# An LSTM with a residual on one core: moving the first groups of products between the plain products, and building the input-weight sums from one another

## The chip, the cores and the metric

The kernel runs on one core of one Trainium2 chip. The metric is the device time of one execution in microseconds (us); the figure for a kernel is the median of its timed runs. Names of the engines: TensorE is PE in the profile, VectorE is DVE, ScalarE is ACT, GpSimd is POOL, SyncE is SP.

## What is computed

The reference is an LSTM over 512 time steps for a batch of 32, with 512 inputs and 512 hidden units, and a residual sum:

```python
def lstm_forward(x, h0, Wx, Wh, b):          # x (32, 512, 512), Wx and Wh (512, 2048)
    xW = jnp.einsum('ntd,dg->ntg', x, Wx) + b
    def step(carry, xw_t):
        prev_h, prev_c = carry
        a = xw_t + prev_h @ Wh
        i, f, o = sigmoid(a[:, :H]), sigmoid(a[:, H:2*H]), sigmoid(a[:, 2*H:3*H])
        g = jnp.tanh(a[:, 3*H:])
        next_c = f * prev_c + i * g
        next_h = o * jnp.tanh(next_c)
        return (next_h, next_c), next_h
    ...
return x + hs
```

All numbers are float32.

## The kernel before

There are two kinds of matmul work. The recurrence, `h_part(k)` (L624), multiplies the state by Wh once per time step and adds into one of two PSUM banks, `gates[0]` and `gates[1]`, which alternate by step. ACT seeds those banks with the input part of the step (`seed_first`, `seed_last`, L611 and L615). `cell(k)` (L637) then makes the new state: sigmoids and tanh on ACT, products on DVE, a transpose of the state on DVE (L659) for which the next recurrence waits.

The input part, x times Wx, is made ahead of time in three ways:

- **Plain products**, `direct(t, bank)` (L557): one time step at full cost, into a whole PSUM bank; `keep_direct` (L573) has DVE add the bias and move the result to SBUF. Steps 0 to 7 and the last 16 steps are made so.
- **Units**, in the head (steps 8 to 39): a unit is eight time steps of one column block of Wx. It is done with seven block products in place of eight (a Strassen-Winograd scheme), each over two halves k. It needs sums of the x blocks (`inner_sums`, L236 to L239, by `prepare`) and sums of four columns of a Wx block (`t_sums`, L160 to L162).
- **Jobs of superblocks**, from step 40 on: 24 steps in a block, 20 jobs each. These use a second, outer scheme that multiplies sums of x blocks by sums of Wx blocks. The Wx sums are constant, so they are made once: `make_factors(n)` (L201 for the additions of blocks, L210 to L213 for the four inner differences), and then stored to DRAM by SP (L207) and fetched again when a job needs them. Fourteen of the twenty are sums of two or more blocks.

The products of units and jobs are spread over **windows**. A unit or job that begins in window w has its products in windows w to w + 4; `products(v)` (L369) issues all products of window v, and `evacuate(v)` moves finished parts out of PSUM: ACT copies (L397, L401, L408, L409, L432) and DVE additions (L404, L410) that read and rewrite the same banks. The 16 units start at windows 0, 1, 2, 3, 4, 5, 6, 8, 9, 11, 12, 14, 15, 17, 18 and 20. Which windows belong to step k is written out by hand:

```python
def windows_of(k):
    if k < 0:
        return [0]
    return [2 * k + 1, 2 * k + 2] if k < 3 else [k + 4]
```

so steps 0, 1 and 2 have two windows each, one behind the other, and every later step has one. In a step, the order of issue is `h_part`, then for each window `evacuate`, `run_due`, `products`, `fetch`, and the cell behind the first window.

DVE's deferrable work (the Wx sums, and in the steady part the x sums) lies in a list sorted by the window in which it is due. `run_due(v, room)` issues what is due, and then what fits into a room given in columns (5000 in the head, an operation costs its columns plus 160). The tiles of Wx sums in the making rotate through a ring of three (`wa`) and a ring of four (`wb`); a tile's buffer is free again when its store has been done.

The order at the start, before step 0: six warm-up matmuls (L745) on zeros, plain products of steps 0 to 3 interleaved over the four quarters of the inputs, the `t_sums` of all eight Wx blocks, the x sums for window 0 (`prepare(0)`), the bias additions of steps 0 to 3, plain products of steps 4 to 7 into four free banks with `run_due(0, 2800)` behind each, the seeds, `products(0)`.

At the end, in the window `FIRST_TAIL - 5`, SP asks for two Wx blocks (0 and 5) again, because their room had been used for other things, and for the last two rows of x (L732 and L119), in one burst.

The whole order is fixed by the program: no scheduler moves an instruction on its engine.

Of the kernel before, what the change touches and what calls it, by code (L numbers as in the profile page):

```python
# [9 lines left out]
F32 = mybir.dt.float32  # L10
# [4 lines left out]
P = 128  # L15
B = 32
T = 512
NJ = 4
G = 4
IFG = 3 * P  # L20
ROW = 8
NROWS = T // ROW
C = 256
# [11 lines left out]
R = len(A_OF)  # L35
# [15 lines left out]
UNITS = [(i, j) for i in range(1, HEAD // ROW) for j in range(NJ)]  # L51


def windows_of(k):

    if k < 0:
        return [0]
    return [2 * k + 1, 2 * k + 2] if k < 3 else [k + 4]


START = windows_of(HEAD - LEAD)[0]
# [14 lines left out]
def kernel(  # L76
# [39 lines left out]
    def load_row(i, a=0, b=ROW):  # L116
        if i not in rows:
            rows[i] = xpool.tile([P, ROW, NJ, B], F32, name=f"row_{i}", tag="row")
        nc.sync.dma_start(  # L119
            out=rows[i][:, a:b].rearrange("p t q b -> p (t q b)"),  # L120
            in_=x[i][:, a * P : b * P],
        )
# [55 lines left out]
    def ring(n, name):  # L178
        return (
            rpool.tile([P, 3, C], F32, name=f"wa_{name}", tag="wa", bufs=3),  # L180
            rpool.tile([P, 4, C], F32, name=f"wb_{name}", tag="wb", bufs=4),
        )

    def make_factors(n):
        tiles = []
        (first, s0), *rest = B_OF[n]
        assert s0 > 0
        v = nc.vector

        def dst(part):  # L190
            if not tiles:
                tiles.extend(ring(n, f"make_{n}"))
            return tiles[1][:, 0:3] if part.start else tiles[0][:, 0:1]

        ops = []
        for part in (slice(0, 1), slice(1, 4)):
            for m, (b, sign) in enumerate(rest):

                def add(part=part, m=m, b=b, fn=v.tensor_add if sign > 0 else v.tensor_sub):
                    to = dst(part)  # L200
                    fn(to, to if m else raw[first][:, part], raw[b][:, part])  # L201

                ops.append(((part.stop - part.start) * C, add))

        def keep():
            for to, part in zip(kept[n], tiles):
                nc.sync.dma_start(out=to, in_=part.rearrange("p n c -> p (n c)"))  # L207

        ops += [
            (C, lambda: v.tensor_sub(tiles[0][:, 1], tiles[1][:, 0], tiles[0][:, 0])),  # L210
            (C, lambda: v.tensor_sub(tiles[1][:, 3], tiles[1][:, 2], tiles[1][:, 0])),
            (C, lambda: v.tensor_sub(tiles[0][:, 2], tiles[1][:, 2], tiles[0][:, 1])),
            (C, lambda: v.tensor_sub(tiles[1][:, 0], tiles[1][:, 1], tiles[0][:, 2])),  # L213
            (0, keep),
        ]
        return ops

    def push_factors():
        done = []
        ops = [op for n in range(R) if len(B_OF[n]) > 1 for op in make_factors(n)]  # L220
# [35 lines left out]
    def run_due(v, room):  # L256

        i = 0
        while i < len(due):
            window, _, columns, fn, ready = due[i]  # L260
            if window > v and (columns + FIXED > room or not ready(v)):
                i += 1
                continue
            assert ready(window)
            due.pop(i)
            fn()
            room -= columns + FIXED
            i = 0
# [283 lines left out]
    def direct(t, bank, qs=range(4)):  # L552
        i, a = divmod(t, ROW)
        for q in qs:
            k, e = divmod(q, 2)
            for j in range(NJ):
                nc.tensor.matmul(  # L557
                    flat(bank)[j * B : (j + 1) * B],
                    rows[i][:, a, q],
                    raw[NJ * k + j][:, 2 * e : 2 * e + 2].rearrange("p n c -> p (n c)"),  # L560
                    start=q == 0,
                    stop=True,
                    skip_group_check=True,
                )

    def keep_direct(t, bank, room=None):
        if room is not None:
            xw[t] = room
        elif t < 4:
            xw[t] = upool.tile([P, G * P], F32, name=f"xw_{t}", tag="xw", bufs=4)  # L570
        else:
            xw[t] = node_free[t - 4].rearrange("p t e b -> p (t e b)")
        nc.vector.tensor_add(xw[t], flat(bank), bias_sb)  # L573
# [144 lines left out]
    def fetch(v):  # L718

        job = jobs.get(v + 2)  # L720
        if job and job.w >= START and len(B_OF[job.kind[1]]) > 1:
            job.ring = [rpool.tile([P, 3, C], F32, name=f"wa_{job.w}", tag="wa", bufs=3), None]
            nc.sync.dma_start(out=job.ring[0].rearrange("p n c -> p (n c)"), in_=kept[job.kind[1]][0])
        job = jobs.get(v)
        if job and job.w >= START and len(B_OF[job.kind[1]]) > 1:
            job.ring[1] = rpool.tile([P, 4, C], F32, name=f"wb_{job.w}", tag="wb", bufs=4)
            nc.sync.dma_start(out=job.ring[1].rearrange("p n c -> p (n c)"), in_=kept[job.kind[1]][1])
        if v == FIRST_TAIL - 5:
            for i in range(8):
                if i not in single:  # L730
                    raw[i] = rpool.tile([P, 4, C], F32, name=f"raw_again_{i}", tag="wb", bufs=4)
                    nc.sync.dma_start(out=raw[i].rearrange("p n c -> p (n c)"), in_=wx[i])  # L732
            for i in range(END // ROW, T // ROW):
                load_row(i)
        sb, rest = divmod(v + 6 - START, PER)
        if v + 6 in UNIT_AT[2 * NJ :: NJ]:
            load_row(3 + UNIT_AT[2 * NJ :: NJ].index(v + 6))
        if rest < MO and 0 <= sb < NSB:
            load_row(HEAD // ROW + MO * sb + (0, 2, 1)[rest])

    with tc.manual_schedule():
        warm = work.tile([P, G, P], F32, name="warm", tag="s")
        nc.scalar.activation(warm[:, 0], c_init, AF.Sigmoid)
        for m in range(6):
            nc.tensor.matmul(  # L745
                pps[0][0:B].rearrange("p n c -> p (n c)"),
                c_init[:, 0:B],
                c_init.unsqueeze(1).to_broadcast([P, 4, P]),
                start=True,
                stop=True,  # L750
            )
# [105 lines left out]
```

## Time and profile before

| | |
|---|---|
| median of 3 runs | 3162.43 us (3160.52 to 3162.44) |
| the profiled execution's own time | 3159.27 us |
| its span, first to last instruction | 3157.5 us |
| mean granted TensorE clock | 0.998 |
| busy: PE, DVE, ACT, POOL | 99%, 70%, 51%, 29% |

The profile is of one execution. Busy shares are of the span. In a timeline row stand the start, the length, engine, line, operation, output and input tiles, shape, the count of instructions merged into the row and, in brackets, the idle time before it and what ended that. A float32 matmul shows as two records.

### The profile page before, as it was taken

The numbers are of one execution on the slowest core, as the hardware profiler recorded it, in microseconds if no ns is written. First come the engines' busy times: TensorE is split into PE (matmuls) and PEld (weight loads), VectorE is DVE, ScalarE is ACT, GpSimd is POOL, SyncE is SP. The second block draws the span as 40 slices with busy tenths as digits, with TensorE's granted clock in tenths as the row PEclk, the third lists the DMA queues.
The fourth block names the chain that finished last, engine by engine and source line by source line (L and its number), as shares of the span: only waits on it lengthen the run. The fifth ranks groups of instructions, "written<-read, shape, count | busy, mean of one in ns | idle before, by whom it ended". The sixth has DMA issues, their size and how long they took to land.

```text
span 3157.5 us, 133431 instructions
## 1 busy us (share of the span) xinstructions
PE 3125.9 (99%) x56620; PEld 2002.8 (63%) x56620; DVE 2198.7 (70%) x6139; ACT 1605.6 (51%) x4842; POOL 915.9 (29%) x1001
## 2 busy tenths in 40 slices
PE   9999999999999999999999999999999999999999
PEld 3666666666666666666666666666666666666544
DVE  7736777777676777777776777776777767677433
ACT  2445555555555555555555555555555555555333
POOL 0122333233233323232332323232333323232320
PEclk9999999999999999999999999999999999999999
DMA  6555666666665756767676757667576667576410
GB/s 237 180 169 187 227 209 207 219 193 227 210 225 186 244 188 216 225 189 227 193 225 207 229 184 240 193 216 226 185 231 199 224 207 236 175 233 195 153 62 25
DMA packets 316085, 631.64 MB, mean 200 GB/s; under 512 B 41952, under 2 KB 107744, under 8 KB 314976
## 3 DMA queue, kind: packets, MB, share of 16 engines
q1 hardware_dynamic: 315344, 623.09, 61.4%
q8 instruction: 446, 7.31, 1.0%
q14 instruction: 151, 1.24, 0.1%
q10 hardware_dynamic: 144, 0.01, 0.0%
HBM read 448.60 MB, written 174.33 MB: 197 GB/s over the span
## 4 chain that ended last, share of the span: by engine, by line
PE 85%; DVE 8%; ACT 3%; DMA 2%; issue 1%; SPq 1%; DVEq 0%; POOL 0%; ACTq 0%; POOLq 0%
PE gates L624 50%; PE pp L369 15%; PE acc L369 14%; PE p L369 5%; DMA xw<-raw_sb 1%; PE pp L557 1%; DMA xw<-slot 1%; DVE node L304 1%; ACT pp L408 1%; SPq L426 1%; DVE wb_make L201 1%; PE acc L557 1%; DVE c L652 1%; ACT ig L653 1%; DVE fc L654 0%
## 5 line engine op out<-in xcount | busy, mean ns | idle before, releaser
L624 PE MATMUL gates<-wh_sb,ht 128*32 128x384 f32 x32704 | 1873.2, 380 | 20.0 <-DVE ht L659 19.3
L624 PEld LDWEIGHTS gates<-wh_sb,ht 128*32 128x32 f32 x32704 | 1120.8, 110 | 804.6 <-issue 672.6
L663 POOL TENSOR_TENSOR oc<-xr,ht 128x128 f32<-128x128 f32 x509 | 299.5, 588 | 2146.6 <-DVE ht L659 2132.5
L605 POOL TENSOR_TENSOR xw<-xw,bias_sb 128x512 f32<-128x512 f32 x488 | 634.1, 1299 | 76.9 <-DMA xw<-xw 36.2
L647 ACT ACTIVATE s<-gates 128x256 f32<-128x256 f32 x512 | 197.7, 386 | 799.2 <-PE gates L624 793.1
L410 DVE TENSOR_TENSOR pp<-acc,p 128x256 f32<-128x256 f32 x396 | 171.0, 432 | 251.4 <-ACT pp L409 237.7
L650 DVE TENSOR_TENSOR fc<-s,c 128x128 f32<-128x128 f32 x511 | 149.9, 293 | 238.7 <-ACT s L647 234.6
L654 DVE TENSOR_TENSOR fc<-s,ig 128x128 f32<-128x128 f32 x512 | 149.5, 292 | 192.7 <-ACT ig L653 192.7
L408 ACT COPY pp<-pu 128x512 f32<-128x512 f32 x396 | 237.1, 599 | 47.8 <-DVE slot L516 18.5
L611 ACT COPY gates<-xw 128x384 f32<-128x384 f32 x492 | 232.7, 473 | 23.0 <-DVE xw L573 21.4
L369 PE MATMUL pp<-wb,node 128*32 128x256 f32 x3040 | 243.6, 379 | 0.0
L649 ACT ACTIVATE s<-gates 128x128 f32<-128x128 f32 x512 | 142.3, 278 | 189.2 <-PE gates L624 189.2
L653 ACT ACTIVATE ig<-c 128x128 f32<-128x128 f32 x512 | 158.6, 310 | 140.8 <-DVE c L652 114.2
L409 ACT COPY pp<-acc 128x256 f32<-128x256 f32 x396 | 142.2, 359 | 142.8 <-DVE slot L516 69.1
L659 DVE STREAM_TRANSPOSE ht<-fc 128x128 f32<-128x128 f32 x511 | 159.1, 311 | 53.8 <-DVE fc L654 0.5
L404 DVE TENSOR_TENSOR pu<-acc,p 128x256 f32<-128x256 f32 x396 | 162.4, 410 | 27.7 <-ACT p L401 27.7
L397 ACT COPY pu<-acc 128x256 f32<-128x256 f32 x396 | 147.3, 372 | 47.3 <-PE acc L369 45.0
L369 PE MATMUL acc<-wa,s 128*32 128x256 f32 x2128 | 170.6, 379 | 0.0
L369 PE MATMUL acc<-wb,s 128*32 128x256 f32 x2128 | 170.5, 379 | 0.0
L369 PE MATMUL pp<-wb,s 128*32 128x256 f32 x2128 | 170.5, 379 | 0.0
L369 PE MATMUL p<-wa,s 128*32 128x256 f32 x2128 | 170.5, 379 | 0.0
L401 ACT COPY p<-p 128x256 f32<-128x256 f32 x396 | 149.6, 378 | 26.7 <-PE p L369 20.5
(144 smaller groups left out, 4072.5 us busy)
## 6 DMA issues: line engine op xcount, KB each, us to landing
wb<-keep_b SPq DMA_DIRECT2D x266, 512.0 KB, 5.4
xw<-xw SPq DMA_DIRECT2D x488, 256.0 KB, 4.0
wa<-keep_a SPq DMA_DIRECT2D x266, 384.0 KB, 4.8
xw<-slot SPq DMA_DIRECT2D x624, 128.0 KB, 3.2
xr<-in_x_dram SPq DMA_DIRECT2D x256, 128.0 KB, 3.1
out_dram<-oc SPq DMA_DIRECT2D x255, 128.0 KB, 2.1
row<-in_x_dram SPq DMA_DIRECT2D x63, 512.0 KB, 6.8
xw<-raw_sb SPq DMA_DIRECT2D x252, 128.0 KB, 3.4
```

What stands on the lines that cost most here:

```text
L369: nc.tensor.matmul(dst[t * B : (t + 1) * B], a[:, t], w, start=s in (1, 5) and m == 0, stop=True, skip_group_check=True,)
L404: nc.vector.tensor_add(job.pu[:, 1], job.acc, job.p5)
L408: nc.scalar.copy(job.pp[0], job.pu)
L410: nc.vector.tensor_add(job.pp[1][:, 1], job.acc, job.p5)
L605: nc.gpsimd.tensor_add(xw[t], xw[t], bias_sb)
L611: nc.scalar.copy(gates[t % 2][:, 0:IFG], xw[t][:, 0:IFG])
L624: nc.tensor.matmul(g[j * B : (j + 1) * B, cols], state["ht"][:, k, :], wh_sb[:, k, j, cols], start=False, stop=True, skip_group_check=True,)
L647: nc.scalar.activation(s[:, 0:2], g[:, 0:2], AF.Sigmoid)
L650: nc.vector.tensor_mul(fc, s[:, 1], state["c"])
L653: nc.scalar.activation(tc_t, c, AF.Tanh)
L659: nc.vector.transpose(ht.rearrange("p q b -> p (q b)"), h)
L663: (nc.gpsimd if t < T - 3 else nc.vector).tensor_add(state["oc"][:, tt % 2], xr[t][:, tt % 2], ht)
```

## The change

- `windows_of(k)` is `[k + 4]` for every step. Windows 0 to 3 are issued ahead of step 0: `products(0)` behind the plain products of step 3, and windows 1, 2 and 3 behind the plain products of steps 4, 5 and 6 (each with its `evacuate`, `run_due` and `fetch`).
- The plain products of steps 4 to 7 go into `gates[0]` and `gates[1]` in turn, not into four other banks. `run_due` there has a room of 2400.
- The x sums of window 0 come after the `t_sums` of five Wx blocks; the other three follow.
- The warm-up has 24 matmuls over four column strips of `pps[2]`, not 6 in one strip of `pps[0]`.
- The Wx sums are built from one another, as a list `B_OPS` written by hand has it: 15 additions of blocks, not 31. A number -1 - n in the list stands for the four inner differences of sum n and its store. The order in which the sums are made and stored changes with it.
- At the end, the two rows of x are asked for in windows `FIRST_TAIL - 10` and `- 8`, the two Wx blocks in `FIRST_TAIL - 5` and `- 3`.

From step 12 or so on up to the reloads the order of the instructions on each engine is the same as before.

```diff
+B_OPS = [
+    (0, "add", 0, 4),
+    (3, "add", 8, 3),
+    (11, "sub", 2, 8),
+    -1,
+    (1, "add", 8 + 3, 7),
+    -1 - 3,
+    (12, "add", 8 + 11, 6),
...
+]
 def windows_of(k):
-    if k < 0:
-        return [0]
-    return [2 * k + 1, 2 * k + 2] if k < 3 else [k + 4]
+    return [k + 4]
...
-    def make_factors(n):
-        tiles = []
-        (first, s0), *rest = B_OF[n]
...
+    def push_factors():
+        v = nc.vector
+        made, ops, done = {}, [], []
+        def outer(n, how, a, b, part):
+            if n not in made:
+                made[n] = ring(n, f"make_{n}")
+            def source(u):
+                if u < 8:
+                    return raw[u][:, part]
+                return made[u - 8][1][:, 0:3] if part.start else made[u - 8][0][:, 0:1]
+            (v.tensor_add if how == "add" else v.tensor_sub)(source(8 + n), source(a), source(b))
...
+        for op in B_OPS:
+            if isinstance(op, int):
+                for z in ((1, 4, 0), (7, 6, 4), (2, 6, 1), (4, 5, 2)):
+                    ops.append((C, lambda n=-1 - op, z=z: inner(n, *z)))
+                ops.append((0, lambda n=-1 - op: keep(n)))
+            else:
+                for part in (slice(0, 1), slice(1, 4)):
+                    ops.append(((part.stop - part.start) * C, lambda op=op, part=part: outer(*op, part)))
...
-        if v == FIRST_TAIL - 5:
-            for i in range(8):
-                if i not in single:
-                    raw[i] = rpool.tile([P, 4, C], F32, name=f"raw_again_{i}", tag="wb", bufs=4)
-                    nc.sync.dma_start(out=raw[i].rearrange("p n c -> p (n c)"), in_=wx[i])
-            for i in range(END // ROW, T // ROW):
-                load_row(i)
+        if v in (FIRST_TAIL - 10, FIRST_TAIL - 8):
+            load_row(END // ROW + (v - FIRST_TAIL + 10) // 2)
+        if v in (FIRST_TAIL - 5, FIRST_TAIL - 3):
+            i = [i for i in range(8) if i not in single][(v - FIRST_TAIL + 5) // 2]
+            raw[i] = rpool.tile([P, 4, C], F32, name=f"raw_again_{i}", tag="wb", bufs=4)
+            nc.sync.dma_start(out=raw[i].rearrange("p n c -> p (n c)"), in_=wx[i])
...
-        for m in range(6):
+        for m in range(6 * NJ):
             nc.tensor.matmul(
-                pps[0][0:B].rearrange("p n c -> p (n c)"),
+                pps[2][m % NJ * B : (m % NJ + 1) * B].rearrange("p n c -> p (n c)"),
...
-        for i in range(8):
+        for i in range(5):
             for op in t_sums(i):
                 op()
         for op in prepare(0):
             op()
+        products(0)
+        for i in range(5, 8):
+            for op in t_sums(i):
+                op()
         push_factors()
         for t in range(4):
             keep_direct(t, firsts[t])
-        for t, bank in zip(range(4, ROW), (pps[2], accs[0], accs[1], p5)):
-            direct(t, bank)
-            run_due(0, 2800)
-            keep_direct(t, bank)
+        for v, t in enumerate(range(4, ROW), 1):
+            direct(t, gates[t % 2])
+            for op in prepare(v):
+                op()
+            if v < 4:
+                evacuate(v)
+            run_due(0, 2400)
+            keep_direct(t, gates[t % 2])
+            if v < 4:
+                products(v)
+                fetch(v)
         seed_first(0)
         seed_last(0)
         seed_first(1)
-        products(0)
-        for op in prepare(1):
-            op()
```

More of the change, by code (lines that the diff above doesn't have):

```diff
@@ L51, with check_sums @@
 UNITS = [(i, j) for i in range(1, HEAD // ROW) for j in range(NJ)]
+B_OPS = [
[6 more added lines that the diff above has]
+    (12, "add", 8 + 11, 6),
+    -1 - 11,
+    -1 - 1,
+    -1 - 12,
+    (4, "add", 1, 5),
+    (10, "add", 8 + 4, 6),
+    -1 - 4,
+    (8, "add", 8 + 10, 2),
+    -1 - 10,
+    (15, "add", 8 + 8, 3),
+    -1 - 8,
+    (17, "add", 8 + 15, 7),
+    -1 - 15,
+    -1 - 17,
+    (5, "add", 0, 3),
+    -1 - 5,
+    (13, "sub", 2, 0),
+    -1 - 13,
+    (19, "add", 5, 6),
+    -1 - 19,
+    (16, "add", 1, 2),
+    (16, "add", 8 + 16, 3),
+    -1 - 16,
+]
+def check_sums():
+    value = {b: {b: 1} for b in range(8)}
+    for op in B_OPS:
+        if isinstance(op, int):
+            continue
+        n, how, a, b = op
+        total = dict(value[a])
+        for block, sign in value[b].items():
+            total[block] = total.get(block, 0) + (sign if how == "add" else -sign)
+        value[8 + n] = {block: sign for block, sign in total.items() if sign}
+    for n, terms in enumerate(B_OF):
+        assert len(terms) == 1 or value[8 + n] == dict(terms)
+check_sums()
 def windows_of(k):
-    if k < 0:
-        return [0]
-    return [2 * k + 1, 2 * k + 2] if k < 3 else [k + 4]
+    return [k + 4]
 START = windows_of(HEAD - LEAD)[0]
@@ L182, in ring @@
         )
-    def make_factors(n):
-        tiles = []
-        (first, s0), *rest = B_OF[n]
-        assert s0 > 0
+    def push_factors():
         v = nc.vector
[L190 to L206, printed above, removed]
-                nc.sync.dma_start(out=to, in_=part.rearrange("p n c -> p (n c)"))
[L209 to L216, printed above, removed]
@@ new lines, in inner, with keep @@
+        def inner(n, to, a, b):
+            to, a, b = (made[n][z // 4][:, z % 4] for z in (to, a, b))
+            v.tensor_sub(to, a, b)
+        def keep(n):
+            for to, part in zip(kept[n], made[n]):
+                nc.sync.dma_start(out=to, in_=part.rearrange("p n c -> p (n c)"))
+        for op in B_OPS:
+            if isinstance(op, int):
+                for z in ((1, 4, 0), (7, 6, 4), (2, 6, 1), (4, 5, 2)):
[4 more added lines that the diff above has]
+                    ops.append(((part.stop - part.start) * C, lambda op=op, part=part: outer(*op, part)))
```

3 lines of the change are left out of this document (removed).

## The prediction

> **What bounds the kernel now.** The page first: its line of engines says that TensorE (PE) is busy 99% of the span. The profiled execution took 3159.27 us with a span of 3157.5, so 1.8 us lie around the span; the median of the three timed runs, 3162.43, is 3.2 above it.
>
> ```profile
> PE 3125.9 (99%) x56620; PEld 2002.8 (63%) x56620; DVE 2198.7 (70%) x6139; ACT 1605.6 (51%) x4842; POOL 915.9 (29%) x1001
> ```
>
> So at most 31.6 us of PE idle can be won, unless PE work goes, and none does: the same matmuls are issued. Second, the waits of PE show who holds it (total, times, longest), and the busy time by stretches shows where (width, PE, PEld, DVE, ACT, POOL busy, then PE's granted clock, DMA share, GB/s).
>
> ```profile
> PE gates L624 <- DVE ht L659: 19.3, 27, 4.4
> PE acc L369 <- DVE pp L410: 5.0, 2, 2.5
> ```
>
> ```profile
> 0.00:140.00 140.00, 130.21 (x1944) 67.12 (x1948) 100.58 (x231) 41.72 (x116) 10.55 (x17) 0.98 0.59 206
> ...
> 300.00:3000.00 2700.00, 2686.87 (x49471) 1755.05 (x49464) 1961.99 (x5490) 1429.86 (x4310) 838.30 (x898) 1.00 0.66 210
> ...
> 48.66:67.57 18.91, 16.41 (x276) 8.91 (x272) 12.93 (x32) 5.42 (x15) 0.46 (x1) 0.91 0.52 168
> ```
>
> In the first 140 us PE idles 9.8 us; in the following 2700 us it idles 13.1, spread thin. The stretch 48.66 to 67.57 has more in it than idle time: its mean clock is 0.91. A finer cut finds the place:
>
> ```profile
> 60.00:62.00 2.00, 2.00 (x20) 0.50 0.29 114
> ```
>
> Third, PE's timeline over the head (start, length, work, idle before it and its releaser). "pp L745" is the warm-up, L557 the plain products, L369 the products of the groups, L624 the recurrence of a step.
>
> ```profile
> 1.05 6.89 PE L745 MATMUL pp<-c_init 128*32 128x512 f32 x11 [1.05 <-DVE c_init L143]
> 7.36 0.63 PE L557 MATMUL gates<-raw_sb,row 128*32 128x512 f32 x3
> ...
> 24.55 0.60 PE L557 MATMUL acc<-raw_sb,row 128*32 128x512 f32 x3
> ...
> 38.28 1.07 PE L369 MATMUL p<-t,s_h 128*32 128x256 f32 x16 [1.57 <-DVE node L573]
> 39.16 3.64 PE L624 MATMUL gates<-wh_sb,h_init 128*32 128x384 f32 x64
> 42.62 1.05 PE L369 MATMUL acc<-t,s_h 128*32 128x256 f32 x16
> ...
> 48.66 3.64 PE L624 MATMUL gates<-wh_sb,ht 128*32 128x384 f32 x64
> ...
> 59.97 1.93 PE L369 MATMUL acc<-t,s_h 128*32 128x256 f32 x16 [2.50 <-DVE pp L410]
> ...
> 67.57 3.63 PE L624 MATMUL gates<-wh_sb,ht 128*32 128x384 f32 x64
> ...
> 87.50 3.64 PE L624 MATMUL gates<-wh_sb,ht 128*32 128x384 f32 x64
> ...
> 96.11 3.66 PE L624 MATMUL gates<-wh_sb,ht 128*32 128x384 f32 x64 [0.66 <-DVE ht L659]
> ...
> 120.83 3.66 PE L624 MATMUL gates<-wh_sb,ht 128*32 128x384 f32 x64 [1.13 <-DVE ht L659]
> ...
> 145.21 3.66 PE L624 MATMUL gates<-wh_sb,ht 128*32 128x384 f32 x64 [1.13 <-DVE ht L659]
> ```
>
> Units of work follow from these starts. Five plain steps lie between 7.36 and 24.55: 3.44 us each. A recurrence is 42.62 - 39.16 = 3.46. Seven products of a group lie between 42.62 and 48.66: 0.863 each.
>
> The recurrence of step 3 starts at 87.50. Between the end of plain step 3 (24.55 - 3.44 = 21.11) and 87.50 lie 66.4 us. The work in them is plain steps 4 to 7 (13.75), three recurrences (10.4) and windows 0 to 6, which hold 2, 3, 4, 6, 7, 7 and 7 products (36 x 0.863 = 31.1): 55.2 us. **So 11.2 us are lost there now**: the wait at 38.28, the two double windows (idle of 2.50 before 59.97 and again in step 2), and half-clock matmuls after each of these two gaps.
>
> What fills a gap of 2.50 is an evacuation with nothing on PE beside it. The chain of waits around the first gap:
>
> ```profile
> 57.54 0.59 ACT slot L432
> 58.13 0.28 ACT pu L397
> 58.40 0.28 ACT p L401
> 58.68 0.49 ACT pp L408
> 59.17 0.29 ACT pp L409
> 59.48 0.45 DVE pp L410
> ```
>
> 2.4 us from end of one window to the next window's first product. In steps with one window this runs beside the recurrence (3.46 us), which is why later steps don't show it.
>
> **The new order, laid out from these units.** Windows 1, 2 and 3 move from steps 0 to 2 ahead of step 0, each behind one plain step; the steps keep one window each. VectorE (DVE) and ScalarE now matter at four places:
>
> ```profile
> 17.01 0.69 DVE L160 TENSOR_TENSOR t<-raw_sb 128x512 f32<-128x512 f32 x1
> ...
> 21.58 0.28 DVE L236 TENSOR_TENSOR s_h<-row 128x128 f32<-128x128 f32 x1
> ...
> 23.44 1.28 DVE L573 TENSOR_TENSOR xw<-gates,bias_sb 128x512 f32<-128x512 f32 x2
> ...
> 89.74 0.43 DVE L410 TENSOR_TENSOR pp<-acc,p 128x256 f32<-128x256 f32 x1 [6.02 <-ACT pp L409]
> ...
> 94.07 0.28 DVE L650 TENSOR_TENSOR fc<-s,c 128x128 f32<-128x128 f32 x1
> ```
>
> ```profile
> L611 ACT COPY gates<-xw 128x384 f32<-128x384 f32 x492 | 232.7, 473 | 23.0 <-DVE xw L573 21.4
> ```
>
> (1) Plain step 4 now goes into a gates bank and so waits for DVE's bias addition of step 0. The factor sums t of blocks 5 to 7 and the eight sums for window 0 change places but stay ahead of it, so it keeps its start of 23.44 and is done near 24.1. PE has done window 0 at 21.11 + 1.73 = 22.84: **a new wait of 1.3 us**. The eight sums now start at 17.01 and read row 1, whose landing is issue plus 11.0:
>
> ```profile
> 3.67 2.62 SPq L119 DMA_DIRECT2D row<-in_x_dram  x2
> ```
>
> ```profile
> row<-in_x_dram SPq DMA_DIRECT2D x1, 512.0 KB, 11.0
> ```
>
> Two issues share 2.62 us; the second, row 1, starts by 5.8 at the latest that leaves it half a microsecond, so it lands near 16.8: in time, with 0.2 to spare; 0.5 late is my bound.
>
> (2) Then PE runs without a wait: plain step 4 to 27.6, window 1 to 30.2, step 5 to 33.6, window 2 to 37.1, step 6 to 40.5, window 3 to 45.7, step 7 to 49.1, recurrence 0 to 52.6. Each evacuation between them lies beside a plain step of 3.44 us, longer than its chain of 2.4; a gates bank alternates, so its bias addition has a window and a plain step's time.
>
> (3) Window 4's evacuation isn't covered fully. ScalarE seeds the gates after the bias addition of step 7 (49.1, 0.2 until the last matmul's end, as a group's 16 records show 1.05 where starts lie 0.86 apart, and 0.7 of its own: 50.0), two copies of at most 0.47, then the chain of 2.4: 53.3, so PE waits 0.7 behind recurrence 0.
>
> (4) The sums built from one another hold tiles longer in a ring of three. The sum that comes right behind the storing of the first finished one takes that one's buffer, so DVE waits for its DMA (the store's landing, least, median, most):
>
> ```profile
> DMA to landing us min/median/max: 2.3/3.0/4.9
> ```
>
> Queued behind this wait on DVE are the bias addition of step 6, window 4's eight sums (23.44 - 21.58 = 1.9 us), four factor operations and the bias addition of step 7, for which the seeds wait. The store can go out near 40.0 (DVE's addition for window 3 must wait for ScalarE's copies after window 2, 37.1, the 0.2, copies of 0.28, 0.49 and 0.29 and its own 0.45: 38.8; three of 0.42 follow), lands by 43.0, and 0.42 + 0.7 + 1.9 + 0.95 + 3 x 0.42 = 5.2 us of work (operation lengths below) bring DVE to 48.2, ahead of plain step 7's end at 49.1. A landing of 4.9 would make it 0.9 late: cost 0 to 0.9, taken as 0 by the median.
>
> With windows 4, 5, 6 and recurrences 1, 2 (21 x 0.863 + 2 x 3.46 = 25.0) recurrence 3 starts at 52.6 + 0.7 + 25.0 = 78.3, not 87.50: **9.2 us won**. The step's own chain keeps up: in step 0 DVE has eight factor operations behind the evacuation (at most 3.9 us by the rows below), to 57.2, and the cell's chain takes 96.11 - 94.07 = 2.04, so the state is there at 59.2; PE is done with window 4 at 59.3. That is nearly no margin.
>
> **Fewer additions.** Sixteen go, each in two pieces:
>
> ```profile
> L201 DVE TENSOR_TENSOR wb_make<-raw_sb 128x768 f32<-128x768 f32 x10 | 9.5, 951 | 0.0
> ...
> L201 DVE TENSOR_TENSOR wa_make<-raw_sb 128x256 f32<-128x256 f32 x10 | 4.2, 418 | 0.0
> ```
>
> 16 x (0.951 + 0.418) = 21.9 us of DVE, but DVE isn't the bound; it counts only where PE waits for the state behind such work, at 96.11, 120.83 and 145.21 (0.66 + 1.13 + 1.13). In step 3 the queue between 90.17 and 94.07 (3.9 us) becomes six small and one large operation, 3.5: 0.4 won. In step 6 (wait before 120.83) it becomes six small and two large, 4.4 us; that is no less than step 3's 3.9, with a shorter window beside it, so between 0 and 1.1, taken as half: 0.6. Ahead of 145.21 (step 9) one operation is left of a whole queue: 1.1. **2.1 us**, between 0 and 2.9.
>
> **Late reloads.** They are asked for in steps near 2937 us, and first used here:
>
> ```profile
> L557 PE MATMUL acc<-raw_again,row x40: 592/592/593, 2972.7 to 3106.8; 128*32 128x512 f32 x40
> ...
> L732 SPq DMA_DIRECT2D raw_again<-in_L_cond_Wx_dram x2: 332/357/382, 2937.3 to 2940.8; - x2
> ...
> DMA to landing us min/median/max: 4.0/4.1/4.1
> ```
>
> Block 5's reload moves two steps later, at most 19.0 us with a recurrence and a full window of seven products in each. 2940.8 + 19.0 + 4.1 is 2963.9, ahead of 2972.7. The row loads go earlier into free buffers. PE waits nowhere near; SP's queue loses a burst that held nobody. Zero; without that margin a step's stall.
>
> **Warm-up.** 24 matmuls over four column strips take the place of six in one. The plain products show that four strips run side by side (a plain step's 32 records in 3.44 us is four per 0.43), so its length stays: zero, at most 0.4 at its end.
>
> **Sum:** 9.2 + 2.1 = 11.3 us off 3159.27 gives 3148.0 in a profiled execution, and off the median 3162.43 gives 3151.1, rounded to 3151.
>
> **The clock rule.** A gap of 2.50 us was followed by clock 0.50; the gap of 1.57 before 38.28 was not (recurrence 0 behind it takes the full-clock 3.46). My waits of 1.3 and 0.7 are under both, so I charge no half clock. The Trainium skill, "TensorE: Matmul & The Clock Gate", What's actually happening, says that the clock falls after an idle window of about 3.4 us, and that the windows run freely. By it the 2.50 gaps would have kept the clock; this trace disagrees. A fall after one of the shorter waits stands among the rivals, priced by rows.
>
> **Rivals.**
> - The additions' saving is worth nothing, since each step takes as much factor work as its room allows until it is used up. For: DVE's queue before the cell is capped by room, not by what is left. Gain 9.2, 3153.2. Chance 0.2.
> - A DVE wait on a store, or row 1, comes late and the clock falls after the new waits: 0.5 + 0.9 more idle and 1.6 for each fall (59.97 to 67.57 is 7.6 us for seven products, not 6.04). Gain 11.3 - 1.4 - 3.2 = 6.7, 3155.7. For: margins of 0.1 to 1.1 us in three places; against: all in one direction is needed. Chance 0.15.
> - Another wait of the new prologue, which before has no row for, eats half: within 0.2% (6.3 us, about what a measurement here can tell from no change). Chance 0.07.
> - Slower: the warm-up's strips don't overlap, as they all stream one operand into one bank. 12 records take it to 7.36 now; 36 more at 0.43 add 15.5 us ahead of all else, net 4.2 slower, 3166.6. It decides from 11.3 us of delay on. Against: plain products share bank and stationary operand and do overlap. Chance 0.04.
>
> The forecast has 0.54. The range 3146 to 3157 takes in the forecast with the additions' upper bound (0.8 more), the two new waits absent (2.0) and 2 for the spread of the three timed runs (3160.52 to 3162.44), and at the other end the first two rivals. Faster by over 0.2%: 0.54 + 0.2 + 0.15, less a little for the second rival's end, 0.87; same 0.07 + 0.02 = 0.09; slower 0.04.
>
> **What would show it.** In the new trace: plain step 4 waiting some 1.3 us for the bias addition; no wait of 2.5; clock 1.00 from 8 us on; recurrence 3 starting at 78 +- 1.5; no wait of PE in step 9. Wrong if recurrence 3 starts after 82, if the warm-up ends after 9, or if PE waits for DVE in steps 0 to 2.

## The result and the profile after

| | before | after |
|---|---|---|
| median | 3162.06 us (3160.52 to 3162.44, 6 runs) | 3145.80 us (3143.66 to 3146.31, 6 runs) |
| profiled execution | 3159.27 | 3145.59 |
| its span | 3157.5 | 3143.8 |

After to before is 0.9948 (95% interval 0.9935 to 0.9961): 16.3 us faster, where 11 were forecast. The median lies 0.2 us under the low end of the range.

The page of the changed kernel, its line of PE, and the waits of PE (total, times, longest):

```profile
PE 3121.6 (99%) x56656; PEld 1999.3 (64%) x56656; DVE 2177.2 (69%) x6107; ACT 1604.4 (51%) x4842; POOL 915.1 (29%) x1001
```

```profile
PE gates L667 <- DVE ht L702: 14.6, 28, 1.7
PE gates L600 <- DVE xw L616: 1.1, 1, 1.1
PE acc L412 <- DVE pp L453: 0.5, 1, 0.5
```

The two waits behind double windows (5.0 us in all) and the one for the last plain product (1.6) are gone; a wait of 1.1 ahead of plain step 4 is new. The waits for the state are 28 (27 before), but the longest is 1.7 where it was 4.4. The stretches show where PE works more densely:

```profile
0.00:140.00 140.00, 137.03 (x2184) 71.65 (x2188) 86.61 (x223) 46.55 (x131) 13.11 (x21) 1.00 0.67 233
...
300.00:3000.00 2700.00, 2688.36 (x49445) 1752.76 (x49441) 1959.18 (x5480) 1427.18 (x4306) 839.61 (x900) 1.00 0.66 210
```

PE's timeline over the head of the changed kernel:

```profile
1.05 7.71 PE L787 MATMUL pp<-c_init 128*32 128x512 f32 x48 [1.05 <-DVE c_init L192]
8.59 1.89 PE L600 MATMUL gates<-raw_sb,row 128*32 128x512 f32 x16
...
25.32 3.64 PE L600 MATMUL gates<-raw_sb,row 128*32 128x512 f32 x32 [1.10 <-DVE xw L616]
...
50.30 3.64 PE L667 MATMUL gates<-wh_sb,h_init 128*32 128x384 f32 x64
...
54.40 1.07 PE L412 MATMUL acc<-t,s_h 128*32 128x256 f32 x16 [0.47 <-DVE pp L453]
...
79.46 3.64 PE L667 MATMUL gates<-wh_sb,ht 128*32 128x384 f32 x64
...
87.23 3.64 PE L667 MATMUL gates<-wh_sb,ht 128*32 128x384 f32 x64
...
111.08 3.66 PE L667 MATMUL gates<-wh_sb,ht 128*32 128x384 f32 x64 [0.36 <-DVE ht L702]
...
133.53 3.66 PE L667 MATMUL gates<-wh_sb,ht 128*32 128x384 f32 x64
```

Recurrence 3 starts at 79.46 (forecast 78.3, before 87.50), recurrence 10 at 133.53 (before 145.21): 8.0 and 11.7 us won. DVE in the same stretch:

```profile
16.20 0.69 DVE L209 TENSOR_TENSOR t<-raw_sb 128x512 f32<-128x512 f32 x1 [0.55 <-DMA raw_sb<-in_L_cond_Wx_dram]
...
18.14 0.29 DVE L279 TENSOR_TENSOR s_h<-row 128x128 f32<-128x128 f32 x1 [0.33 <-DMA row<-in_x_dram]
...
24.58 1.28 DVE L616 TENSOR_TENSOR xw<-gates,bias_sb 128x512 f32<-128x512 f32 x2
...
43.21 0.42 DVE L246 TENSOR_TENSOR wa_make<-wa_make,raw_sb 128x256 f32<-128x256 f32 x1 [1.99 <-DMA keep_a<-wa_make]
...
50.55 0.69 DVE L616 TENSOR_TENSOR node<-gates,bias_sb 128x512 f32<-128x512 f32 x1 [2.57 <-PE gates L600]
```

DVE waits 0.55 us for a Wx block and 0.33 for row 1; these are most of what makes its bias additions start at 24.58 and not at 23.44. The wait on a store (1.99, before 43.21) is there as foreseen and hidden: DVE is still 2.57 early for plain step 7.

The rest of the gain is at the other end. The table gives the time between the same two states (starts of the state's transposition, L659 before and L702 after, read from the traces; "state k" is the one that step k makes).

| us | start to state 10 | to state 40 | state 40 to 470 | 470 to 478 | 478 to 510 |
|---|---|---|---|---|---|
| before | 150.06 | 345.38 | 2583.65 | 50.37 | 169.99 |
| after | 138.38 | 333.27 | 2586.99 | 45.45 | 170.00 |
| difference | -11.7 | -12.1 | +3.3 | -4.9 | 0.0 |

The forecast had -11.3 up to state 40, and nothing in the other columns. The steps 40 to 470 hold the same instructions in the same order in both kernels, but for the two row loads, which the changed kernel asks for at 2899 and 2913 us; from state 465 to state 470 both take 29.82 us, so these cost nothing. The +3.3 is within the scatter of that stretch (below); with it the two profiles stand 13.7 us apart, where the medians stand 16.3 apart.

What stood at steps 470 to 478 in the kernel before: SP's queue, DVE, PE, and the landing times of the store of `slot` (least, median, most, issue to landing). `slot` is a buffer in which DVE adds up finished parts; SP stores it to DRAM in four pieces.

```profile
2937.31 3.81 SPq L732 DMA_DIRECT2D raw_again<-in_L_cond_Wx_dram  x2
2941.18 2.35 SPq L119 DMA_DIRECT2D row<-in_x_dram  x2
2943.63 0.38 SPq L602 DMA_DIRECT2D xw<-xw  x1
2944.10 2.64 SPq L426 DMA_DIRECT2D xw<-slot  x4
```

```profile
2952.26 0.69 DVE L516 TENSOR_TENSOR slot<-t,pp 128x512 f32<-128x512 f32 x1 [3.12 <-DMA xw<-slot]
```

```profile
2956.89 5.35 PE L624 MATMUL gates<-wh_sb,ht 128*32 128x384 f32 x64 [4.36 <-DVE ht L659]
```

```profile
DMA to landing us min/median/max: 6.0/6.5/7.1
```

The four reloads (two Wx blocks, two rows of x) fill SP's queue and the DMA engines (busy at 0.98 from 2946 to 2949 us); the store behind them lands 6 to 7 us after its issue, its last piece at 2952.14. DVE's addition into the next `slot` has to wait for that, 3.12 us, and starts 0.12 later; the cell's products are queued behind it on DVE. So PE waits 4.36 us for the state, and it resumes with a fallen clock (0.68, then 0.50, in the next two stretches of 2 us; 5.35 us for a recurrence, not 3.66). In the changed kernel the same store has only one Wx block near it:

```profile
2928.55 0.38 SPq L776 DMA_DIRECT2D raw_again<-in_L_cond_Wx_dram  x1
...
2933.75 1.74 SPq L469 DMA_DIRECT2D xw<-slot  x4
```

```profile
DMA to landing us min/median/max: 1.9/2.2/2.3
```

```profile
2940.28 0.67 DVE L559 TENSOR_TENSOR slot<-t,pp 128x512 f32<-128x512 f32 x1
```

```profile
2944.89 3.66 PE L667 MATMUL gates<-wh_sb,ht 128*32 128x384 f32 x64 [1.14 <-DVE ht L702]
```

The store lands in 2.2 us, DVE's addition has no wait in front of it, and PE waits 1.14 us and keeps the full clock. Counted from the start of the DVE additions just ahead of the store (2942.42 and 2933.64), its last piece lands after 9.7 us in the kernel before and after 3.6 in the changed one. Of the 6.1 us between them 2.3 is a later issue on SP and 3.8 a longer landing.

### The profile page after: what moved, and what is told of

Its sections match the earlier page's. It is cut to its first block, busy times and chain, and to the rows that moved or that the text cites. A ratio compares the mean times of both kernels' runs of the same rounds, so it can differ in the third digit from the quotient of the medians.

```text
span 3143.8 us, 133477 instructions
## 1 busy us (share of the span) xinstructions
PE 3121.6 (99%) x56656; PEld 1999.3 (64%) x56656; DVE 2177.2 (69%) x6107; ACT 1604.4 (51%) x4842; POOL 915.1 (29%) x1001
## 4 chain that ended last, share of the span: by engine, by line
PE 89%; DVE 6%; DMA 2%; ACT 2%; issue 1%; SPq 1%; DVEq 0%; POOL 0%
PE gates L667 51%; PE pp L412 15%; PE acc L412 15%; PE p L412 5%; PE pp L600 1%; DMA xw<-xw 1%; DVE node L347 1%; PE acc L600 1%; ACT pp L451 1%; DMA xw<-slot 0%; DMA xw<-raw_sb 0%; ACT ig L696 0%; PE gates L600 0%; DVE c L695 0%; DVE fc L697 0%
## 5 line engine op out<-in xcount | busy, mean ns | idle before, releaser
L702 DVE STREAM_TRANSPOSE ht<-fc 128x128 f32<-128x128 f32 x511 | 159.1, 311 | 55.5 <-DVE fc L697 2.7
L695 DVE TENSOR_TENSOR c<-fc,ig 128x128 f32<-128x128 f32 x512 | 150.5, 294 | 17.7
```

The costliest lines, as they stand in the source:

```text
L702: nc.vector.transpose(ht.rearrange("p q b -> p (q b)"), h)
```

## The experiments

Medians are of runs that share their sessions with the kernel before (3160.75 us over 27 runs there, 3160.79 and 3160.98 in the later ones). Single times are of one execution.

**The reloads alone**, in the kernel before:

```diff
-        if v == FIRST_TAIL - 5:
-            ...            # two blocks and two rows
+        if v in (FIRST_TAIL - 10, FIRST_TAIL - 8):
+            load_row(...)  # one row in each
+        if v in (FIRST_TAIL - 5, FIRST_TAIL - 3):
+            ...            # one block in each
```

> The kernel before with the late reloads alone spread as in the change. Theory (the burst of two blocks and two rows holds up a store, the store holds up a DVE addition that stands ahead of the cell, and PE waits 4.4 us near step 475 and then runs at half clock): 4 to 6 us faster than before, 3156 to 3158, and no wait of PE over 2 us in the last hundred steps. Rival (the reloads cost nothing, and what the change won beyond the head is the scatter between executions): within 1.5 us of before, and the late wait either stays or another of its size stands near it.

Measured: 3157.12 us, ratio 0.9988 (0.9980 to 0.9997), some 3.6 us. The store lands in 2.2 us and the wait of 4.36 is gone, but steps 470 to 478 take 48.00, not 45.45: at step 477 a wait of 2.71 us, which the theory had excluded, takes some of it back, and the clock falls behind it (0.50 in the 2 us from 2968.82 on). What made that wait was a product on DVE that took 1.35 us instead of 0.29:

```profile
2965.72 1.35 DVE L650 TENSOR_TENSOR fc<-s,c 128x128 f32<-128x128 f32 x1 [2.83 <-ACT s L647]
```

```profile
2965.65 1.26 POOL L605 TENSOR_TENSOR xw<-xw,bias_sb 128x512 f32<-128x512 f32 x1 [2.80 <-DMA out_dram<-oc]
```

It starts 0.07 us behind the start of an addition on GpSimd and ends 0.16 behind that one's end. In this trace 4 of the 512 products of this kind start within a GpSimd addition; these take 1.08 to 1.35 us, and the other 508 at most 0.30. Whether one falls on a step where PE has no slack hangs on the timing of the execution: of the eight profiles of this study with blocks or rows spread, six take 45.45 to 45.95 us for steps 470 to 478, this one 48.00 and one more 47.59 (below). The changed kernel's 45.45 is so in part luck, of 2.1 to 2.5 us. This profiled execution took 3160.37, 3.2 above the median of its kernel.

**The burst put back** into the changed kernel (the diff above, reversed):

> The changed kernel with the late reloads again in one burst. Theory: the wait of some 4 us near step 475 is back, and the gain on the kernel before falls to what the head gives, 11 to 12 us (3150 to 3151). Rival: as fast as the changed kernel, 16 us ahead of before, with no wait over 2 us there.

Measured: 3149.07 us, ratio 0.9963 (0.9951 to 0.9976), 3.3 us above the changed kernel's median. Each against the kernel before of its own session, it gains 11.7 us where the changed kernel gains 16.3, 4.6 less. Steps 470 to 478 take 49.85, 4.4 more. The landing of the store, DVE's addition and PE follow. The row puts DVE's wait down to a PE product, but the same addition ran ahead of that product in the changed kernel; the last piece of the store landed at 2941.71, 0.12 before the addition's start, as in the kernel before:

```profile
DMA to landing us min/median/max: 5.7/7.2/7.5
```

```profile
2941.83 0.69 DVE L559 TENSOR_TENSOR slot<-t,pp 128x512 f32<-128x512 f32 x1 [2.60 <-PE pp L412]
```

```profile
2946.46 5.36 PE L667 MATMUL gates<-wh_sb,ht 128*32 128x384 f32 x64 [3.83 <-DVE ht L702]
```

Its head is that of the changed kernel (state 40 at 333.24). So the theory holds: the reloads are worth what the tail shows, and the head is worth its 12 us without them.

**Part of the burst.** First both Wx blocks in one window, rows early (two loads ahead of the store); then both rows and one block in one window, the other block later (three loads):

```diff
+        if v in (FIRST_TAIL - 10, FIRST_TAIL - 8): load_row(...)      # first kernel
+        if v == FIRST_TAIL - 5: ...                                   # both blocks
```

```diff
+        if v in (FIRST_TAIL - 5, FIRST_TAIL - 3): ...                 # second kernel, one block each
+        if v == FIRST_TAIL - 5: load_row(...), load_row(...)
```

> The changed kernel with its two row loads early, but both blocks again asked for together in the window of the old burst. Theory: the wait near step 475 grows with what stands in the queue ahead of the store, so half the burst gives half the wait or less: 0 to 2 us more in steps 470 to 478 than the changed kernel's 45.45. Rival: the two blocks are what matters (they go ahead of the step's input load and of the store at once): 49 to 50 us in these steps.

> The changed kernel with the blocks spread, but both row loads again in the window of the old burst, behind the first block. Theory: three transfers ahead of the store in place of four, 1 to 3 us more in steps 470 to 478 than 45.45. Rival: the rows cost nothing, 45.5.

Measured: 3144.63 and 3144.52 us, 470 to 478 in 45.45 and 45.46. The store's landing, in the first and in the second:

```profile
DMA to landing us min/median/max: 4.1/4.4/4.5
```

```profile
DMA to landing us min/median/max: 4.7/5.0/5.1
```

Two or three of the loads already double the landing time, but they cost nothing: DVE's additions show no wait there. That is the low end of the first theory; the second expected 1 to 3 us and missed, its rival holds. With all four reloads the store lands in 5.7 to 7.5 us, and that is too late. Either half of the edit would have done, by one execution of each.

**The kernel before, once more**, for what its profile repeats:

> The kernel before, unchanged, once more with a profile: what differs between two executions of one program. Theory: the head (state of step 40 at 345.4) and steps 470 to 478 (about 50) repeat within 0.5 us, while steps 40 to 470 scatter by some us (2583.65 before, 2586.99 in the changed kernel). Rival: the late wait scatters as much, and its loss in the changed kernel was chance.

Measured: 3161.32 us. The tail's waits are there again (longest 4.7, 470 to 478 in 51.25). Steps 40 to 470 took 2586.89 where the first profile had 2583.65, so 3.2 us come and go there with nothing changed; over all profiles of this study that stretch lies between 2583.65 and 2588.14. The head did not repeat as expected: state 40 came at 343.33, 2.0 earlier than in the first profile. Of these, 1.5 are the clock: behind the first double window PE waited 2.50 us, as before, but the granted clock was 1.00 from 60 to 62 us, where the first profile has 0.50. Against this execution the head of the changed kernel gains 10.1 us, not 12.1.

**The order alone**: the windows, the plain products' banks, the x sums' place and the warm-up of the changed kernel, with the old sums and the burst.

```diff
+    return [k + 4]
...                        # products(1..3) behind plain steps 4 to 6, run_due(0, 2400)
```

> The kernel before with the new order of the head alone (windows 1 to 3 between the plain products, warm-up on four strips), the old Wx sums and the burst. Theory: PE's double windows go, recurrence 3 starts at 79.5 as in the changed kernel, and the waits ahead of steps 4, 7 and 10 stay near 0.7 to 1.1 us: 8 to 9 us faster than before, near 3154. Rival: the new order needs the lighter sums, since DVE has the same room in the prologue and more to do later: under 5 us faster, with new waits of PE for the state in steps 1 to 9.

Measured: 3157.32 us, ratio 0.9990 (0.9981 to 0.9999). Recurrence 3 starts at 79.52, as in the changed kernel; then the gain goes: state 10 comes only 3.2 us earlier than before and state 40 only 2.6. The waits that take it (PE's timeline):

```profile
87.89 3.66 PE L623 MATMUL gates<-wh_sb,ht 128*32 128x384 f32 x64 [0.39 <-DVE ht L658]
...
113.74 5.35 PE L623 MATMUL gates<-wh_sb,ht 128*32 128x384 f32 x64 [2.25 <-DVE ht L658]
...
159.31 3.66 PE L623 MATMUL gates<-wh_sb,ht 128*32 128x384 f32 x64 [2.17 <-DVE ht L658]
```

So the rival holds. DVE has more windows ahead of step 0 but does less of its list in each (room 2400, where the steps have 5000), and the 31 additions run into the steps: of the 118 operations of the sums 24 lie ahead of state 0 on DVE (28 in the kernel before), and the last is in step 12. The changed kernel has 86 in all and is through with them in step 9.

**The order with room**: the same, but with a room of 4200 behind each plain product.

```diff
-            run_due(0, 2400)
+            run_due(0, 4200)
```

> The new order with the old sums, as before, but with a room of 4200 columns behind each plain product and not 2400. Theory (the order alone is given back since three windows, and with them three turns of DVE's list, lie ahead of the steps with half the room, so that more old sums are left to steps 3 to 12): with 37 operations ahead of step 0 instead of 24, the waits for the state in steps 3 to 12 (0.39, 2.25, 0.85, 1.39, 2.17 without it) shrink to under 4 us together, and the state of step 10 is there 2 to 4 us earlier than at 146.9. Rival: the prologue has no idle DVE time to use, its bias additions come late, and what is won later is lost ahead of step 0.

Measured: 3151.39 us, ratio 0.9974 (0.9964 to 0.9985). It went as the theory says: 37 operations of the sums lie ahead of state 0; state 10 is at 142.84, 4.1 earlier, and state 40 at 336.26: of the 12.1 us of the head 9.1 are there with the old sums. The longest wait after step 3 in the head is 1.19. The kernel with the new sums and the same burst has state 40 at 333.24: the sums add 3.0 us (2.3 in the medians).

**The sums alone**, in the old order:

```diff
-    def make_factors(n): ...
+    B_OPS = [...]          # and push_factors as in the changed kernel
```

> The kernel before with the Wx sums alone built from one another (15 additions). Theory: DVE has 22 us less to do, but only the queues ahead of the cell in light windows count: 2 to 3.5 us faster than before, near 3159.5, with the double windows and the late wait as before. Rival (each step takes as much as its room allows): within 1 us of before, and the waits ahead of steps 4, 7 and 10 stay. Third: the wait for a store's buffer in the ring of three shows in the head without a plain product to hide it, and it is slower by 1 to 3 us.

Measured: 3163.05 us, ratio 1.0005 (0.9996 to 1.0014): no change that is clear of noise (the medians stand 2.3 apart, this one the slower). The third of the expected mechanisms shows. In the old order DVE has no plain step's worth of other work between a store and the sum that reuses its buffer, so the two waits on stores stand in front of the bias additions, and PE stands behind these:

```profile
33.53 0.43 DVE L247 TENSOR_TENSOR wa_make<-wa_make,raw_sb 128x256 f32<-128x256 f32 x1 [1.52 <-DMA keep_a<-wa_make]
...
39.27 0.43 DVE L247 TENSOR_TENSOR wa_make<-wa_make,raw_sb 128x256 f32<-128x256 f32 x1 [2.39 <-DMA keep_a<-wa_make]
```

```profile
41.56 1.94 PE L413 MATMUL p<-t,s_h 128*32 128x256 f32 x16 [4.65 <-DVE node L617]
43.27 5.22 PE L668 MATMUL gates<-wh_sb,h_init 128*32 128x384 f32 x64
```

PE waits 4.65 us where it waited 1.57 and goes on at half clock; state 0 is 5.5 us late (49.63 for 44.11). By state 10 nearly all of it has been won back (150.37 for 150.06): 3.9 us between recurrences 3 and 10, where the waits for the state are gone, and 1.7 by chance. The two double windows still cost PE 2.50 us each, but only behind the first of them did the clock fall:

```profile
65.67 1.07 PE L413 MATMUL acc<-t,s_h 128*32 128x256 f32 x16 [2.50 <-DVE pp L454]
...
67.87 1.95 PE L413 MATMUL acc<-t,s_h 128*32 128x256 f32 x16
...
85.60 1.07 PE L413 MATMUL acc<-t,s_h 128*32 128x256 f32 x16 [2.50 <-DVE pp L454]
...
87.35 1.05 PE L413 MATMUL acc<-t,s_h 128*32 128x256 f32 x16
```

**The prologue of the changed kernel.** A warm-up of nine matmuls, six in one strip and one in each other; then, apart from that, the bias addition of step 0 put ahead of the last sums of Wx columns:

```diff
-        for m in range(6 * NJ):
+        for m in (0, 0, 0, 0, 0, 0, 1, 2, 3):
```

```diff
         for i in range(5, 8):
+            if i == 5:
+                keep_direct(0, firsts[0])
             for op in t_sums(i):
```

> The changed kernel with a shorter warm-up: six matmuls in one column strip and one in each of the three others, so that every strip of the bank is begun. Theory: the plain products start about 1 us earlier (7.4 to 7.8), but DVE, whose factor sums follow the landing of the inputs, still makes plain step 4 start at 25.3: the wait before it grows to about 2 us and recurrence 3 stays at 79.5, or at 81 if that wait lowers the clock. Rival: the later end of the long warm-up is what PE pays, and recurrence 3 starts at 78.4.

> The changed kernel with the bias addition of step 0 alone put ahead of two of DVE's factor sums. Theory: the wait of 1.10 before plain step 4 goes and nothing else moves, recurrence 3 starts at 78.4. Rival: recurrence 3 at 79.5, since another wait grows by as much.

Measured: 3146.67 and 3144.17 us, recurrence 3 at 78.52 and 77.50 (79.46). In the first, plain step 4 starts 0.95 us earlier, and so does the bias addition for which it waits:

```profile
23.63 1.28 DVE L616 TENSOR_TENSOR xw<-gates,bias_sb 128x512 f32<-128x512 f32 x2
```

```profile
24.37 3.64 PE L600 MATMUL gates<-raw_sb,row 128*32 128x512 f32 x32 [0.23 <-DVE xw L616]
```

In this run DVE waited for neither the Wx block nor row 1. PE came to step 4 at 24.14 (24.37 less its wait of 0.23), in the changed kernel at 24.22 (25.32 less 1.10). So that gain is DVE's, and the short warm-up brought next to nothing (0.08): the number is near the rival's, the cause is not. In the second run, earlier than its theory's 78.4, the wait ahead of plain step 4 is gone, which is 1.1 of its 1.96; 0.67 is an earlier end of the same warm-up (7.92 for 8.59): its matmuls ran at 8 to 12 records a microsecond up to 6 us in the changed kernel's trace and up to 5 in this one, and at 12 to 16 after that.

**Window 4's evacuation ahead of the seeds**, on top of the bias addition:

```diff
-            if v < 4:
-                evacuate(v)
+            evacuate(v)            # window 4 too, ahead of the seeds
...
-                taken = evacuate(v)
+                taken = evacuate(v) if k else 0
```

> The changed kernel with the bias addition of step 0 ahead of two of DVE's factor sums, and with the evacuation of window 4 ahead of the seeds, beside plain step 7. Theory: both waits of PE that the new head has (1.10 before plain step 4, 0.47 before window 4) go, recurrence 3 starts at 77.9 and not at 79.5, the rest as it was: 1.5 us off the changed kernel, 3144 to 3145, which is less than executions scatter. Rival: DVE's other work comes later in exchange, and a wait for the state or for the bias addition of step 7 takes their place; recurrence 3 at 79 or later.

Measured: 3146.44 us, ratio 0.9956 (0.9944 to 0.9969). The wait of 0.47 behind recurrence 0 becomes one of 1.51 inside it, for the seeds that come later on ACT; recurrence 3 starts at 78.51 (77.9 expected), the wait ahead of recurrence 7 is 1.01 where the changed kernel has 0.36, and state 10 is at 138.38, where the changed kernel has it. It gives back what the bias addition won.

**Bias addition and short warm-up together** (both diffs of the prologue):

> The changed kernel with the two edits of the prologue that each moved its head forward: the bias addition of step 0 ahead of the last two sums of T strips, and the warm-up in nine products instead of 24 (six in one strip, one in each other). Theory (the plain products of step 4 wait for nothing but PE's own order once the bias addition is early, so that an earlier end of the warm-up passes through to the recurrences): warm-up over by 8.1 us, no wait before the plain products of step 4, recurrence 3 at 77.0 to 77.6 us (79.46 in the changed kernel, 78.52 and 77.50 with either edit), the median 3143 to 3145 us with a median of the kernel before at 3160.75, ratio 0.994 to 0.995. Rival (both edits take away the same wait, so that together they bring no more than one, and the steps in between find DVE late): recurrence 3 at 77.5 to 78.5 us with a wait of 0.3 us or more after one of the products of the first 80 us, and a median of 3145 to 3146 us, as without the edits.

Measured: 3146.14 us, ratio 0.9955 (0.9941 to 0.9968). The head went as the theory says, but the time is the rival's. Recurrence 3 starts at 77.35, 0.15 ahead of the bias addition alone: the strip that still has six warm-up matmuls sets the pace. State 10 is at 136.29, 2.1 us ahead of the changed kernel, and in the profiled execution the tail loses it: 470 to 478 takes 47.59. It is the collision of the reloads' run again, on DVE, POOL and PE:

```profile
2950.82 0.76 DVE L693 TENSOR_TENSOR fc<-s,c 128x128 f32<-128x128 f32 x1 [2.83 <-ACT s L690]
```

```profile
2950.14 1.28 POOL L648 TENSOR_TENSOR xw<-xw,bias_sb 128x512 f32<-128x512 f32 x1 [2.20 <-DMA xw<-slot]
```

```profile
2953.33 5.31 PE L667 MATMUL gates<-wh_sb,ht 128*32 128x384 f32 x64 [2.12 <-DVE ht L702]
```

No version of this study is faster than the changed kernel by more than the scatter.

## Why the prediction was outside its range

**The step that failed is "Late reloads: zero".** The Wx blocks and rows themselves do land long before their use, as it said. But it looked for who waits for the reloads, and not for what is queued behind them: the store of `slot`, DVE's addition, the cell's products on DVE, the recurrence. The sentence "SP's queue loses a burst that held nobody" was the wrong one. The sign stood in a quoted row: a longest wait for the state of 4.4 us, which the prediction never placed. Measured: 4.9 us between the two profiles, 4.4 with the burst put back (4.6 in the medians, each against its own session).

**The head was right in its size**: 11.3 forecast, 12.1 at state 40 (10.1 against the second profile of the kernel before). That is in part luck, as one term was too high by 1.2 us and the other too low by 1.5. By terms:

- New order, 9.2: recurrence 3 is 8.0 earlier, 1.2 less. What holds it is the bias addition of step 0, for which plain step 4 waits: it is 1.14 late, 0.88 of that by the two inputs (row 1 by 0.33, within the bound of 0.5; the Wx block was not thought of). In the run where both were in time recurrence 3 started at 78.52, forecast 78.3. The wait ahead of plain step 4 is 1.10 (1.3 forecast), because PE came late too, at 24.22 and not at 22.84. The one behind recurrence 0 is 0.47 (0.7). The store's wait was hidden, as taken.
- Warm-up, "zero, at most 0.4 at its end": the forecast counted from 7.36, where three strips began; the strip with the six matmuls was still at its last one then (row below), and went on 0.43 later, at 8.21. The new warm-up is over at 8.59, 0.4 later than that, and at 7.92 in another run. Hidden behind DVE either way.
- Fewer additions, 2.1 (0 to 2.9): between recurrences 3 and 10 it is 3.6, above the bound. The three waits it listed (2.92) shrank to one of 0.36, which gives 3.0 by the starts of the recurrences: a wait costs up to 0.2 more than its row says, because the row counts it from the end of the last matmul, 0.2 behind the point where the next one would have started. Another 0.6 is a fourth wait, ahead of recurrence 9, which the prediction did not list (row below) and which is gone. With the new order on both sides, the sums are worth 3.0 at state 40, so the rival that they are worth nothing is out.
- No wait of 2.5, no half clock in the head's steps, no wait of PE in step 9: as forecast. PE does wait for DVE in step 0, 0.47 us, which was named as a sign of being wrong; the prediction had itself priced that wait at 0.7.

The fourth wait, in the kernel before:

```profile
137.82 3.66 PE L624 MATMUL gates<-wh_sb,ht 128*32 128x384 f32 x64 [0.38 <-DVE ht L659]
```

**The terms don't add up from parts run alone.** Reloads alone give -3.6 us, the order alone -3.4, the sums alone +2.3: together -4.7, where the whole gives -16.3. The order needs DVE's list to be shorter or its room larger, or it hands its gain to the steps; the sums need the plain steps of the new order to hide their stores. The prediction added 9.2 and 2.1 as if each stood by itself; the total came out because both were there.

**The clock rule** held for the short waits: no fall behind 1.10 and 0.47. That the clock does fall behind 2.50 is not certain: of eight such waits in four profiles of the old order, six were followed by a fall and two were not (the second profile of the kernel before, and the sums alone). So of the 11.2 us that the prediction counts as lost in the kernel before, about 1.6 come and go at each double window.

With 4.9 for the reloads and 12.1 for the head, 3159.27 - 17.0 = 3142.3; the 3.3 more in steps 40 to 470 bring the profiled execution back to 3145.59.

The row of the kernel before for the warm-up:

```profile
7.78 0.59 PE L745 MATMUL pp<-c_init 128*32 128x512 f32 x1
```

## What to carry to other kernels

Place every long wait of the waits view on the timeline before a term is set to zero: the longest one here was worth 4 to 5 us and sat in one step at the end. For a burst of transfers, ask what is issued behind it on the same queue and who waits for that one's landing, not only when the burst's own data is used. Price the parts of a change together when one fills the time that another empties: here the order and the lighter sums were worth 12 us together, and one by one a gain of 3.4 us and a loss of 2.3 that is not clear of noise.

## What the runs showed of the hardware

- DMA landing under load: a store of four pieces of 128 KB landed in 2.2 us with one load of 512 KB issued 5.2 us ahead of it, in 4.4 and 5.0 with two and three such loads, and in 6.5 and 7.2 with four (medians of the pieces).
- A DVE product of 128x128 took 0.29 us, but 0.76 and 1.35 when it started within an addition on GpSimd, and ended 0.16 us behind that one both times (rows above). The Trainium skill, "SBUF — State Buffer", SBUF: two separate sides, describes an exclusive port lock between a DVE operation with two SBUF inputs and a GpSimd operation that reads SBUF; these rows agree with it.
- The clock fell behind waits of 2.12, 2.25 and 2.71 us, and not behind 2.11 (step 477 with the short warm-up) and 2.17. Behind waits of 2.50 it fell six times of eight, and in the row at 65.67 above only after 0.9 us of work at full speed. So between 2.1 and 2.5 us the length alone does not decide. The Trainium skill, "TensorE: Matmul & The Clock Gate", What's actually happening, has activity windows that run freely, by which the place of a wait could decide; that agrees, but no run here tests it. Its length of about 3.4 us doesn't: the falls named here came behind shorter waits.
